# A fused two-layer graph network: tiles that went ahead copied graph by graph, and adj's transposes moved in front of conv1

## The chip, the cores and the metric

The kernel runs on one core of a Trainium2 chip. The metric is the device time of one execution, from the first to the last instruction with what the launch adds around it, in microseconds (us). The core has five engines that work side by side, each on its own list of instructions in order: PE (matrix products and transposes; its weight loads are listed apart as PEld), DVE (vector work), ACT (activations and copies), POOL (vector work and some DMAs) and SP (which issues most DMAs). They meet only through semaphores.

## What is computed

There are 64 graphs of 256 nodes with 256 features each, all in fp32. Layer 0 normalises the adjacency and applies one linear map; layer 1 has a convolution branch over the nodes, a message branch over a distance kernel, and a GRU cell that joins them. Both end in a residual and a layernorm.

```python
# layer 0
deg = adj.sum(-1);  d = where(deg != 0, deg, 1) ** -0.5
a_plus = d[:, :, None] * adj * d[:, None, :] + max(alpha, 1e-10) * eye(N)
x = layernorm(x + (a_plus @ x) @ W.T + b)
# layer 1
h = relu(bn1(conv1(x)))                      # 1 tap: a 256x256 product
h = bn2(conv2(h))                            # 17 taps along the nodes
x_conv = relu(h + x)
s = x @ w_se.T + b_se                        # 3 columns
A = exp(-(|s_n|^2 + |s_m|^2 - 2 s_n.s_m))
msg = relu(x @ w_msg.T + b_msg)
x_nmp = (A * adj) @ msg                      # adj is the mask of layer 1
x = layernorm(x + GRU(cat(x_conv, x_nmp), x))
```

## The kernel before

**Stages.** The 64 graphs are taken in four quarters of 16. Per graph, `layer0` (L335 to 409) makes adj's row sums (ACT), its transposes (`p_adjT`, PE, L367; copied by ACT L368), puts alpha times the degree on the diagonal (DVE L370), scales x by the inverse root of the degree (ACT L380), then makes `hT` (L388) and `p_out` (L398), adds the residual (DVE L403) and takes the layernorm. `layer1` (L411 to 500) transposes the result (`p_x1T`, L419, copied by ACT L420 into `xn`), makes `conv1` together with the three distance columns (`p_conv`, L428), the message product (`p_msg`, L449), the forward transform of the convolution branch (`p_dft`, L463), the distance kernel (`p_rows`, `dist_l`, `dist_r`, `p_dist`, `aT`, L476 to 489) and the aggregation (`p_nmp`, L494). Layer 0 of graph g+2 is woven into layer 1 of graph g.

**The 17-tap convolution** is done through a transform with 48 real coefficients per tile of 32 nodes. The forward transform of all 16 graphs of a quarter lies in one large SBUF tile, `VM` (128 x 48 x 256; `V` is its view by frequency, feature half and tile). `products` then multiplies each frequency by its weights on PE and writes the results back in place, and the transform back also runs in place, on DVE, as a list of small steps: `real_transform`, `complex_begin` and at last `complex_end`, whose steps are called the end steps below. Each of its sixteen `output` pieces ends with a store of 256 KB, `xc_d`, that SP issues (L705). The gates of the quarter read these stores later (`xc_g`, L742).

**Going ahead.** While a quarter's products and its transform back are under way, `VM` is taken. So that PE has something to do, the first graphs of the next quarter go ahead: twelve of them during quarter 0, six during quarters 1 and 2. Their forward transforms go to a second tile, `V2`. When the transform back is done, ACT copies `V2` into `V` in four copies of 12 frequencies each (L1031), and the rest of the graphs, here graphs 28 to 31 for quarter 0, write `V` at once. During quarters 1 to 3 PE also has the gates of the quarter before that were left over (`late`).

**Order.** A scheduler keeps each engine's instructions as the Python program issues them, except for pieces that `issue_after` ties to an instruction. `paced(main, other, rate)` does that for the end steps: after each instruction that called `mark`, it adds `rate` and issues a whole number of steps of `other` behind that instruction. There are six marks per graph: two residual steps L403, two bias steps L431, the message bias L452 and the `aT` product L489. `graphs` walks through the seven pieces of `layer1`, and after each it gives the stages named in `PLACES` one step: piece 0 (after `p_x1T`'s copy) gives to `other`, pieces 1, 4 and 5 to layer 0 of a later graph. In the stages where twelve graphs go ahead `other` is empty.

PSUM has four buffers for these products, used in turn. `V2` lives in a pool of its own that is closed after quarter 0's copies; the gates' tiles take its memory, so the gates' first loads cannot start before the copies have ended.

Of the kernel before, what the change touches and what calls it, by code (L numbers as in the profile page):

```python
# [26 lines left out]
def kernel(  # L27
# [380 lines left out]
        nc.scalar.dma_start(x1_d[g // Q][g % Q].rearrange("(c p) d -> p c d", p=P), x1)  # L408
        yield

    def layer1(g, V, place):  # L411

        x1, adjT = X1.pop(g), ADJT.pop(g)
        xn = work.tile([P, 2 * DCH, N], F32, name="xn")
        x1T = xn[:, :DCH]
        p = bank("p_x1T").rearrange("p (k n) -> p k n", k=DCH)
        for k in range(DCH):
            for c in range(NCH):
                nc.tensor.transpose(p[:, k, c * P : (c + 1) * P], x1[:, c, k * P : (k + 1) * P], ident)  # L419
        nc.scalar.copy(x1T, p)  # L420

        yield

        h = work.tile([P, NCH, D + NSE], F32, name="h", bufs=1)
        for c in range(NCH):
            p = bank("p_conv1")[:, : D + NSE]
            for k in range(DCH):
                nc.tensor.matmul(  # L428
                    p, x1T[:, k, c * P : (c + 1) * P], wc1[:, k, :], start=k == 0, stop=k == DCH - 1
                )  # L430
            mark(nc.vector.tensor_tensor(h[:, c, :], p, bc1, op=ALU.add))  # L431
        nc.scalar.activation(h[:, :, :D], h[:, :, :D], AF.Relu)  # L432

        s3 = h[:, :, D:]
        cols = scols.rearrange("p c (q r) -> p c q r", r=32)
        nc.vector.tensor_copy(cols[:, :, :, :NSE], s3.unsqueeze(2).to_broadcast([P, NCH, 4, NSE]))
        sq3 = small.tile([P, NCH, NSE], F32, name="sq3")
        nc.vector.scalar_tensor_tensor(sq3, s3, -1.0, s3, op0=ALU.mult, op1=ALU.mult)
        nsq = small.tile([P, NCH], F32, name="nsq")
        nc.vector.tensor_reduce(nsq, sq3, AX.X, ALU.add)  # L440
        nc.vector.tensor_scalar(
            cols[:, :, 2:4, NSE], nsq.unsqueeze(2).to_broadcast([P, NCH, 2]), 0.5, None, op0=ALU.mult
        )
        yield
        msg = work.tile([P, NCH, D], F32, name="msg", bufs=1)
        p = bank("p_msg").rearrange("p (c d) -> p c d", c=NCH)
        for c in range(NCH):
            for k in range(DCH):
                nc.tensor.matmul(  # L449
                    p[:, c, :], x1T[:, k, c * P : (c + 1) * P], wmsg[:, k, :], start=k == 0, stop=k == DCH - 1  # L450
                )
        mark(nc.vector.tensor_tensor(msg, p, bmsg_t.unsqueeze(1).to_broadcast([P, NCH, D]), op=ALU.add))  # L452
        nc.scalar.activation(msg, msg, AF.Relu)
        yield


        mid = GT // 2
        for k in range(DCH):
            p = bank("p_dft")

            for c, t0, t1 in ((0, 0, mid + 1), (1, mid - 1, GT)):
                first = t0 + 1 - c * mid
                nc.tensor.matmul(  # L463
                    p[:, t0 * FL : t1 * FL], h[:, c, k * P : (k + 1) * P],
                    fwd[:, first : first + t1 - t0, :].rearrange("p t f -> p (t f)"),
                    start=c == 0, stop=True, skip_group_check=c == 1,
                )
            nc.scalar.copy(
                V[:, :, k, place * GT : (place + 1) * GT],
                p[:, : GT * FL].rearrange("p (t f) -> p f t", f=FL),  # L470
            )

        yield
        p = bank("p_rows")
        for c in range(NCH):
            nc.tensor.transpose(p[:, c * P : (c + 1) * P], scols[:, c, :], ident)  # L476
        dl = work.tile([64, N], F32, name="dist_l", bufs=1)
        nc.scalar.copy(dl, p[0:64, :N])
        dr = work.tile([64, N], F32, name="dist_r", bufs=1)
        nc.vector.tensor_copy(dr, p[64:P, :N])  # L480
        yield

        aT = work.tile([P, NCH, 2, P], F32, name="aT", bufs=1)
        for c in range(NCH):
            rows = slice(32 * c, 32 * c + 32)
            p = bank("p_dist")[:, :N]
            nc.tensor.matmul(p, dl[rows, c * P : (c + 1) * P], dr[rows, :], start=True, stop=True)
            nc.scalar.activation(aT[:, c].rearrange("p n q -> p (n q)"), p, AF.Exp, bias=nsq[:, c : c + 1], scale=2.0)  # L488
        mark(nc.vector.tensor_mul(aT, aT, adjT[:, :, 0:3:2, :]))  # L489
        yield  # L490
        p = bank("p_nmp").rearrange("p (k n) -> p k n", k=DCH)
        for k in range(DCH):
            for mc in range(NCH):
                nc.tensor.matmul(  # L494
                    p[:, k, :], msg[:, mc, k * P : (k + 1) * P], aT[:, mc].rearrange("p n q -> p (n q)"),
                    start=mc == 0, stop=mc == NCH - 1,
                )
        nc.scalar.copy(xn[:, DCH:], p)
        nc.scalar.dma_start(xn_d[g], xn)
        yield  # L500
# [3 lines left out]

    VM = freq.tile([P, FL, D], F32, name="VM")
    V, M = VM.rearrange("p f (k q) -> p f k q", k=DCH), VM

    def load_u(n, i):
        u = ustream.tile([P, DCH, D], F32, name="u")
# [362 lines left out]
    def chain(*stages):  # L872
        for stage in stages:
            yield from stage
# [13 lines left out]
    def run(stage):  # L888
        for _ in stage:
            pass  # L890
# [15 lines left out]

    PLACES = (("other",), ("layer0",), (), (), ("layer0",), ("other", "layer0"), ())

    def graphs(first, part, V, others):


        for i in part:
            load(first + i + 3)
            given = {"layer0": layer0(first + i + 2) if first + i + 2 < B else iter(()), "other": others[i]}
            for piece, _ in enumerate(layer1(first + i, V, i)):
                yield
                for name in PLACES[piece]:
                    if next(given[name], "end") != "end":
                        yield
            yield from given["other"]  # L920

    with tc.tile_pool(name="setup", bufs=1) as setup:
        load_taps(setup, 0)
# [27 lines left out]
        more_weights = gate_weights()  # L951
        others = [weights(setup, i, scale2) for i in range(NPARTS)]
        others += [take(more_weights, 1) for i in range(NPARTS, Q)]
        run(graphs(0, range(Q), V, others))
        bih_t = setup.tile([P, 3 * D], F32, name="bih", tag="taps", bufs=2)
        nc.sync.dma_start(bih_t, bcast_rows(b_ih, 3 * D))
        bhh_t = setup.tile([P, 3 * D], F32, name="bhh", tag="taps", bufs=2)
# [9 lines left out]
    def open_ahead(graphs):  # L967

        scope = ExitStack()
        pool = scope.enter_context(tc.tile_pool(name="ahead", bufs=1))  # L970
        return scope, graphs, pool.tile([P, FL, DCH, graphs * GT], F32, name="V2")
# [17 lines left out]
    def nothing():  # L989
        return iter(())  # L990

    RATES = (1.2, 0.85, 0.85, 1.35)


    scope, AHEAD, V2 = open_ahead(12)
    late = nothing()
    for q in range(NQ):
        first = (q + 1) * Q
        more = q + 1 < NQ
        end = complex_end(q)  # L1000
        if more:
            if q:
                others = [take(late, 3 if i % 3 == 0 else 2) for i in range(AHEAD)]
            else:
                others = [nothing() for _ in range(AHEAD)]
            begin = graphs(first, range(AHEAD), V2, others)
        sums(0)
        real = real_transform()
        for step in range(STEPS):
            if step < 4:  # L1010
                run(products(step))
            else:
                run(merge(products(step), take(real, 1)))
                run(complex_begin(step))
            if q:
                run(take(late, (0, 1, 1, 1, 1, 1, 2, 1, 2, 1, 2, 1)[step] if more else step % 2))
            else:
                run(take(begin, 3))
        run(real)
        if not q:  # L1020
            run(paced(begin, end, RATES[q]))
        elif more:
            run(paced(chain(merge(take(late, 20), take(begin, 6), 3), begin), end, RATES[q]))
        else:
            run(paced(late, end, RATES[q]))
            run(end)
        if more:
            run(late)
            run(end)
            for f in range(0, FL, 12):  # L1030
                nc.scalar.copy(V[:, f : f + 12, :, : AHEAD * GT], V2[:, f : f + 12])  # L1031
            if q == 0:
                scope.close()
                gate = ctx.enter_context(tc.tile_pool(name="gate", bufs=2))
            early = gates(q, range(EARLY))
            others = [take(early, 5 if q == 0 else 2) for _ in range(Q)]
            run(graphs(first, range(AHEAD, Q), V, others))
            run(early)
            if q == 0:
                scope, AHEAD, V2 = open_ahead(6)  # L1040
                ctx.enter_context(scope)
            late = gates(q, range(EARLY, Q))
        else:
            run(gates(q, range(Q)))
# [53 lines left out]
```

## Time and profile before

| | us |
|---|---|
| median of three runs | 2169.46 (2168.36 to 2170.78) |
| the profiled execution | 2174.33 |
| its span, first to last instruction | 2172.5 |
| mean granted TensorE clock | 0.989 of full speed |

The stages of the span, with the time in which PE was busy:

| stretch, us | what runs | PE busy |
|---|---|---|
| 0 to 540 | setup, the first quarter's graphs, its products and transform back | 489.74 of 540 |
| 540 to 700 | first gates, graphs 29 to 31, on to the second quarter's products | 153.44 of 160 |
| 700 to 1000 | second quarter, its transform back and copies (968 to 974) at the end | 289.02 of 300 |
| 1000 to 1300 | the same on to the third quarter | 296.14 of 300 |
| 1300 to 1700 | its transform back, on to the fourth | 386.44 of 400 |
| 1700 to 1940 | the fourth quarter's transform back beside gates | 226.12 of 240 |
| 1940 to 2172 | the last gates | 223.11 of 232 |

Graph 28, the first after those that went ahead in quarter 0, has its `p_conv` at 529.61 us; the last store of quarter 0's transform is issued at 519.92, and the first gate load at 529.10. The twelve graphs that go ahead are 16 to 27.

In a timeline a line has the start, the duration, the engine, the line of the kernel, the operation, what it writes and reads with its shape, the number of instructions in the group, and in brackets the idle time just before it with the engine and line that ended it. In a table of windows the columns are the busy time and instruction count of each engine in the stretch, then the granted clock of PE, the share of DMA time and the rate in GB/s. Releasers are worked out from semaphores: where several were waited for, the last is named.

### The profile page before, as it was taken

Reading aid. Unit: us, or ns where it says so; the run is one execution under the profiler, and the core shown is the slowest. Engines: PE = TensorE matmul, PEld = TensorE weight load, DVE = VectorE, ACT = ScalarE, POOL = GpSimd, SP = SyncE. Lnnn points to the kernel's source line nnn. Section 1 sums busy time; section 2 is a strip of 40 time slices with the busy share of each in tenths; the row PEclk is TensorE's granted clock in tenths of the full one; section 3 lists DMA queues with packets and bytes.
Section 4 is the critical chain, followed back from the end, with each engine's and each line's share of the span. In section 5 each row is a group of like instructions: output and inputs, shape, how many; then the busy total and the mean of one; then the engine's idle time right before and its main releaser. Section 6 shows DMA issues by size and latency. Waiting matters only on the chain. (4 is left out here: it accounts for less than half of the span.)

```text
span 2172.5 us, 29034 instructions
## 1 busy us (share of the span) xinstructions
PE 2064.0 (95%) x9805; PEld 1748.4 (80%) x9805; DVE 1550.7 (71%) x3691; ACT 834.3 (38%) x1847; POOL 664.2 (31%) x640
## 2 busy tenths in 40 slices
PE   7999999887999999999999999899999998999998
PEld 5788788776788887788888888778888887788887
DVE  5555568785568798775556989775555889977776
ACT  4566643455331122455453122346543112222222
POOL 2444310211431233313222133323231123444442
PEclk9999999999999999999999999999999999999999
DMA  4765656434337644344335754334334844444442
GB/s 129 223 194 178 216 185 207 154 125 141 97 112 226 194 123 122 107 119 121 104 99 175 208 163 116 110 117 132 101 97 124 250 117 122 120 123 107 112 101 60
DMA packets 251182, 305.65 MB, mean 141 GB/s; under 512 B 18174, under 2 KB 229714, under 8 KB 251034
## 3 DMA queue, kind: packets, MB, share of 16 engines
q1 hardware_dynamic: 183530, 200.46, 30.4%
q10 hardware_dynamic: 44480, 67.39, 8.7%
q0 software_dynamic: 23024, 35.95, 8.6%
q8 instruction: 78, 1.28, 0.2%
q14 instruction: 70, 0.57, 0.1%
HBM read 200.62 MB, written 103.06 MB: 140 GB/s over the span
## 5 line engine op out<-in xcount | busy, mean ns | idle before, releaser
L833 PE MATMUL p_n<-wn,inputs 128*128 128x256 f32 x1536 | 355.9, 385 | 11.0 <-DVE first L809 10.6
L796 PE MATMUL p_rz<-wrz,sums 128*128 128x256 f32 x1536 | 350.9, 382 | 3.2 <-POOL sums L775 2.3
L833 PEld LDWEIGHTS p_n<-wn,inputs 128*128 128x128 f32 x1536 | 289.1, 192 | 58.1 <-DVE first L809 14.5
L796 PEld LDWEIGHTS p_rz<-wrz,sums 128*128 128x128 f32 x1536 | 290.7, 191 | 48.2 <-issue 5.9
L796 PE MATMUL p_rz<-wrz,inputs 128*128 128x256 f32 x1152 | 271.7, 379 | 0.4 <-ACT inputs L766 0.4
L314 POOL TENSOR_TENSOR ln_rs<-ln_rs,neg_half 128x2 f32<-128x2 f32 x129 | 101.2, 784 | 527.9 <-DVE ln_rs L313 417.4
L796 PEld LDWEIGHTS p_rz<-wrz,inputs 128*128 128x128 f32 x1152 | 217.5, 190 | 30.3 <-ACT inputs L766 1.0
L845 ACT ACTIVATE nn<-gn 128x256 f32<-128x256 f32 x128 | 53.2, 416 | 333.2 <-DVE gn L842 333.0
L518 PE MATMUL p_k<-u,VM 128*128 128x256 f32 x736 | 175.3, 380 | 4.1 <-DMA u<-ud 3.3
L775 POOL TENSOR_TENSOR sums<-inputs 128x384 f32<-128x384 f32 x64 | 67.8, 1059 | 335.1 <-ACT inputs L766 327.0
L358 POOL TENSOR_TENSOR dis<-deg,neg_half 128x2 f32<-128x2 f32 x64 | 46.5, 726 | 402.6 <-DVE deg L356 395.6
L324 ACT ACTIVATE x_g<-x_g,ln_mr,ln_rs 128x256 f32<-128x256 f32 x128 | 70.0, 593 | 245.6 <-DVE ln_mr L322 242.0
L518 PEld LDWEIGHTS p_k<-u,VM 128*128 128x128 f32 x736 | 138.1, 190 | 25.7 <-DMA u<-ud 3.4
L428 PE MATMUL p_conv<-wc,xn 128*128 128x259 f32 x512 | 128.8, 394 | 19.6 <-ACT xn L420 18.5
L388 PE MATMUL p_hT<-adjT,x 128*128 128x256 f32 x512 | 126.6, 390 | 9.5 <-DVE msg L452 4.9
L381 POOL TENSOR_TENSOR x_t<-x_t,b_t 128x512 f32<-128x512 f32 x64 | 86.4, 1350 | 146.7 <-ACT x L380 89.3
L463 PE MATMUL p_dft<-fwd,h 128*128 128x240 f32 x512 | 117.8, 373 | 13.9 <-ACT h L432 13.0
L428 PEld LDWEIGHTS p_conv<-wc,xn 128*128 128x128 f32 x512 | 97.1, 194 | 39.8 <-ACT xn L420 24.1
L489 DVE TENSOR_TENSOR aT<-aT,adjT 128x512 f32<-128x512 f32 x64 | 44.3, 692 | 115.3 <-ACT aT L488 115.3
L398 PE MATMUL p_out<-w,hT 128*128 128x256 f32 x512 | 123.9, 385 | 2.5 <-ACT hT L393 2.1
L449 PE MATMUL p_msg<-wmsg,xn 128*128 128x256 f32 x512 | 121.3, 379 | 0.0
L494 PE MATMUL p_nmp<-aT,msg 128*128 128x256 f32 x512 | 121.1, 379 | 0.2 <-DVE aT L489 0.2
(154 smaller groups left out, 3894.9 us busy)
## 6 DMA issues: line engine op xcount, KB each, us to landing
u<-ud SPq DMA_DIRECT2D x284, 256.0 KB
xn_d<-xn ACTq DMA_DIRECT2D x64, 512.0 KB
inputs<-xn_d SPq DMA_DIRECT2D x64, 512.0 KB
ud<-u_set POOLq DMA_DIRECT2D x39, 480.0 KB, 6.2
adj_t<-in_adj_dram SPq DMA_DIRECT2D x64, 256.0 KB
x_t<-in_x_dram SPq DMA_DIRECT2D x64, 256.0 KB
x_d<-x ACTq DMA_DIRECT2D x64, 256.0 KB
xc_d<-VM SPq DMA_DIRECT2D x64, 256.0 KB
```

Source lines behind the costliest of these rows:

```text
L314: nc.gpsimd.tensor_tensor(rs[:, : len(chunks)], rs[:, : len(chunks)], neg_half[:, : len(chunks)], op=ALU.pow)
L324: nc.scalar.activation(y[:, c, :], y[:, c, :], AF.Identity, bias=mr[:, c : c + 1], scale=rs[:, c : c + 1])
L381: nc.gpsimd.tensor_tensor(x_t, x_t, b0_t.unsqueeze(1).to_broadcast([P, NCH, D]), op=ALU.add)
L388: nc.tensor.matmul(p[:, k, :], x1[:, mc, k * P : (k + 1) * P], adjT[:, mc, 1 - mc : 3 - mc, :].rearrange("p n q -> p (n q)"), start=mc == ...
L398: nc.tensor.matmul(p[:, c, :], hT[:, k, c * P : (c + 1) * P], w0[:, k, :], start=k == 0, stop=k == DCH - 1)
L428: nc.tensor.matmul(p, x1T[:, k, c * P : (c + 1) * P], wc1[:, k, :], start=k == 0, stop=k == DCH - 1)
L449: nc.tensor.matmul(p[:, c, :], x1T[:, k, c * P : (c + 1) * P], wmsg[:, k, :], start=k == 0, stop=k == DCH - 1)
L463: nc.tensor.matmul(p[:, t0 * FL : t1 * FL], h[:, c, k * P : (k + 1) * P], fwd[:, first : first + t1 - t0, :].rearrange("p t f -> p (t f)") ...
L494: nc.tensor.matmul(p[:, k, :], msg[:, mc, k * P : (k + 1) * P], aT[:, mc].rearrange("p n q -> p (n q)"), start=mc == 0, stop=mc == NCH - 1,)
L518: nc.tensor.matmul(p[:, j * D : (j + 1) * D], v[:, k, :], u[:, k, :], start=k == 0, stop=k == DCH - 1)
L796: nc.tensor.matmul(p[:, j * D : (j + 1) * D], a[:, k], wrz[:, b, k], start=k == 0, stop=k == HALF - 1)
L833: nc.tensor.matmul(p[:, o * D : (o + 1) * D], lhsT, w, start=j == 0, stop=j == len(part) - 1)
```

## The change

Three things change. First, `V2` is copied graph by graph: a new generator, `copies`, has one ACT copy per graph that wrote to `V2`, and it is chained to the end steps, so that `paced` places its copies as it places those. `TILES[0]` says which tile `layer1` writes its forward transform to; `copies` sets it to `V` when it starts, so a graph that comes to its transform afterwards writes `V` directly, and `AWAY` lists the graphs that did not. In the order that results, quarter 0 has eleven copies (graph 27 writes `V`), and quarters 1 and 2 five each. Second, the rates of the end steps in quarters 0, 1 and 2 rise, from 1.2, .85, .85 to 1.4, .9, .9. Third, `graphs` takes layer 0's first piece (row sums, transposes, diagonal, scale) after piece 0 where `other` has nothing there, instead of after piece 1. That moves it in front of `conv1` for the twelve graphs during quarter 0 and for no others. The number of instructions changes on ACT alone, by nine more.

```diff
-    def layer1(g, V, place):
+    def layer1(g, place):
...
         mid = GT // 2
+        if TILES[0] is not V:
+            AWAY.append(place)
         for k in range(DCH):
...
             nc.scalar.copy(
-                V[:, :, k, place * GT : (place + 1) * GT],
+                TILES[0][:, :, k, place * GT : (place + 1) * GT],
...
     V, M = VM.rearrange("p f (k q) -> p f k q", k=DCH), VM
+    TILES, AWAY = [V], []
...
-    def graphs(first, part, V, others):
+    def graphs(first, part, others):
         for i in part:
             load(first + i + 3)
-            given = {"layer0": layer0(first + i + 2) if first + i + 2 < B else iter(()), "other": others[i]}
-            for piece, _ in enumerate(layer1(first + i, V, i)):
+            zero = layer0(first + i + 2) if first + i + 2 < B else iter(())
+            begun = False
+            for piece, _ in enumerate(layer1(first + i, i)):
                 yield
                 for name in PLACES[piece]:
-                    if next(given[name], "end") != "end":
+                    if name == "other" and next(others[i], "end") != "end":
                         yield
-            yield from given["other"]
+                    elif piece == 0:
+                        begun = next(zero, "end") != "end"
+                        yield
+                    elif name == "layer0" and not (piece == 1 and begun) and next(zero, "end") != "end":
+                        yield
+            yield from others[i]
...
-    RATES = (1.2, 0.85, 0.85, 1.35)
+    RATES = (1.4, 0.9, 0.9, 1.35)
...
+    def copies(V2):
+        waiting = list(AWAY)
+        AWAY.clear()
+        TILES[0] = V
+        for i in waiting:
+            nc.scalar.copy(V[:, :, :, i * GT : (i + 1) * GT], V2[:, :, :, i * GT : (i + 1) * GT])
+            yield
...
-        end = complex_end(q)
+        end = chain(complex_end(q), copies(V2) if more else iter(()))
...
-            begin = graphs(first, range(AHEAD), V2, others)
+            TILES[0] = V2
+            begin = graphs(first, range(AHEAD), others)
...
             run(late)
             run(end)
-            for f in range(0, FL, 12):
-                nc.scalar.copy(V[:, f : f + 12, :, : AHEAD * GT], V2[:, f : f + 12])
```

## The prediction

> **What bounds the kernel now.** I read the page's busy shares first, then busy time by stage, then the waits of PE and of DVE in the stage that changes, then the timelines at its end.
>
> ```profile
> span 2172.5 us, 29034 instructions
> ## 1 busy us (share of the span) xinstructions
> PE 2064.0 (95%) x9805; PEld 1748.4 (80%) x9805; DVE 1550.7 (71%) x3691; ACT 834.3 (38%) x1847; POOL 664.2 (31%) x640
> ```
>
> PE sets the time: 108.5 us of 2172.5 are left to gain, and an edit to ACT's copies or to DVE's order counts only where PE stands still. Windows by stage, 402 to 521.4 us being the main loop of quarter 0 and 521.4 to 543 the seam behind it:
>
> ```profile
> core 0: us, PE busy (x) PEld busy (x) DVE busy (x) ACT busy (x) POOL busy (x), PEclk, DMA share, GB/s
> 288.00:402.00 114.00, 111.34 (x535) 94.96 (x534) 86.37 (x195) 40.53 (x89) 11.00 (x12) 1.00 0.66 210
> 402.00:521.40 119.40, 103.12 (x498) 81.58 (x497) 95.65 (x287) 67.79 (x154) 24.84 (x24) 1.00 0.38 122
> 521.40:543.00 21.60, 13.93 (x63) 11.32 (x62) 5.83 (x22) 12.84 (x22) 5.12 (x5) 0.84 0.67 192
> ```
>
> PE lacks 16.3 us in the stage and 7.7 in the seam, and the seam's clock is 0.84. The waits between 400 and 522 us (engine line waited for: total, times, longest), of PE and of DVE:
>
> ```profile
> PE p_conv L428 <- ACT xn L420: 5.8, 8, 0.7
> PE p_dist L487 <- DVE dist_r L480: 2.5, 4, 0.8
> PE p_hT L388 <- DVE adjT L370: 2.3, 2, 1.5
> PE p_hT L388 <- DVE msg L452: 1.9, 2, 1.1
> ...
> DVE aT L489 <- ACT aT L488: 16.4, 9, 2.8
> DVE ln_mr L322 <- POOL ln_rs L314: 4.9, 8, 0.7
> DVE dist_r L480 <- ACT dist_l L478: 3.0, 4, 1.0
> ```
>
> PE waits for DVE in three places; DVE never waits for PE directly, only for short round trips. So DVE, 95.65 of 119.4 us busy and idle only in such trips (24.3 in all), carries this stage, and PE's 5.8 us before p_conv are mostly slack that it would spend a little later. The seam, on PE and then ACT (start, duration, group, idle before and its releaser):
>
> ```profile
> 517.82 1.99 PE L398 MATMUL p_out<-w,hT 128*128 128x256 f32 x8 [1.33 <-ACT hT L393]
> ...
> 521.38 0.60 PE L419 MATMUL p_x1T<-ident,x 128*128 128x128 f32 x4
> 529.61 3.59 PE L428 MATMUL p_conv<-wc,xn 128*128 128x259 f32 x8 [7.63 <-ACT xn L420]
> 533.03 0.60 PE L367 MATMUL p_adjT<-ident,adj_t 128*128 128x128 f32 x4
> ```
>
> ```profile
> 515.17 2.12 ACT L1031 COPY VM<-V 128x2304 f32<-128x2304 f32 x1
> ...
> 520.07 2.10 ACT L1031 COPY VM<-V 128x2304 f32<-128x2304 f32 x1
> ...
> 524.95 4.12 ACT L1031 COPY VM<-V 128x2304 f32<-128x2304 f32 x2 [0.58 <-ACT x L324]
> 528.98 0.58 ACT L420 COPY xn<-p_x1T 128x512 f32<-128x512 f32 x1
> ```
>
> PE stands 7.63 us because xn of graph 28 is queued behind the last two block copies. The conv then starts its successor 3.42 us later instead of 1.86 (403.36 to 405.22, 418.44 to 420.30): 1.56 us lost to the lower clock.
>
> **What the Trainium skill says.** "TensorE: Matmul & The Clock Gate", Part 1, *What's actually happening*: PE falls to half clock after an idle window of about 3.4 us and needs about that much busy time to return; the window runs free. The trace agrees (granted clock .50 just after the 7.63), and shows .54 after a wait of only 1.90 at 549.76 us, while waits of 1.5 and 1.62 left it whole. The specification table of that page gives ScalarE a strict in-order queue: a copy that waits holds everything behind it, as in the seam. "ScalarE: Activation LUTs", *What ACT_TABLE_LOAD costs*: 186 ns + 0.833 ns per element for an ACTIVATE without pointers. The trace's copies agree: 512 elements 0.58, 2304 elements 2.12. "DMA: Bandwidth & Descriptors", *Anatomy of one DMA*, puts most of a transfer's fixed cost into the wait for the write's receipt (written of POOL's DMAs); here a 256 KB load that SP issued at 529.10 let POOL go at 532.12, so I take 3.0 us from issue to landing for the output stores too.
>
> **The change part by part.**
>
> *Copies by graph and faster end steps, quarter 0.* Before, 4 copies of 12 frequencies follow the transform back. After, 11 copies of one graph do (128x768, estimate 186 + 640 = 0.83 us each); graph 27, the twelfth, writes V at once. ACT's sum is 9.1 us against 8.3, so the point is place, not work. The end steps on DVE finish one graph earlier: 16 of them, 0.35 us apart in the timeline, 5.6 us, move ahead of dist_r of graph 26. That stood at 500.35; some 1.6 us of the 5.6 fall into waits for POOL ln_rs (0.6 each), so it comes at 504.35, just behind the last end step. Then:
> - Each copy covers all frequencies, so the first waits for all of DVE's last steps and for the last stores, to about 504.4 + 3.0 = 507.4; before, only the third copy did. Behind it on ACT stand hT, the two aT, layer 0's scales and xn. It ends at 508.2, hT at 508.75, and p_out, which stood at 502.05, starts there: PE, +4.0 late from dist_r, waits some 2.5 us more.
> - conv of graph 27 comes at 514.05 instead of 506.93, 7.1 late. Graph 27 now has no end steps, so PE sets it: 12.9 us. Further copies stand ahead of its msg and DFT copies (3 and 2, each 0.83, partly in ACT's idle time): p_dist waits an estimated 2.35, p_nmp 0.4.
> - conv of graph 28: 514.05 + 12.9 + 2.75 = 529.7, against 529.61. The stall is cut into pieces rather than removed, since DVE had to do its 5.6 us of end steps in any case and PE has nothing else to fill with.
> - What goes for certain is the half clock after 7.63 us: −1.56. Two waits of 2.3 to 2.5 us may bring it back, between 0 and +3.4; I take +0.6.
> - Gate loads start 3.5 us earlier (copies end at 525.6, not 529.07). p_xcT waited for nothing at 543.16, so 0. Its successor's 1.90 us wait for POOL's sums at 549.76 stays.
>
> Sum: +0.1 − 1.56 + 0.6 = −0.9.
>
> *adj's transposes between x1T and conv1.* This happens for 12 graphs, those that go ahead in quarter 0. In the 8 with a 0.73 us gap before p_conv, transposes of 0.44 fill it: −3.5 at most, nothing where DVE is late anyway. ACT now takes adjT's copy and the two L380 scales ahead of relu h, and DVE its two L370 ahead of scols: h by 0.25 to 0.75 later, for a p_dft that waited 1.19 once in this stage. Bounds −3.5 and +1.5; I take −0.3, for the first graphs only, where DVE has no end steps queued. No PE instruction is added.
>
> *Quarters 1 and 2.* Each has 5 copies (4.2 us) instead of 4 of 1152 (4.4). Before, they cost PE nothing (968.12 and 971.43 us), as late gate matmuls fill PE; so 0, with +1.5 each if that fill is gone. The rate of .9 for .85 puts 4 more end steps, 1.4 us, ahead of the dist_r that PE already waits 4.87 us for at 854.99; .7 to 1.3 of it falls into ln_rs waits, so +0.4. In return end steps finish earlier, and waits of .31 (945.9) and .45 (982.3) go: −0.76. Net −0.4 each, −1.5 to +2.0. Quarter 3 is untouched.
>
> *Total.* −0.9 − 0.3 − 0.8 = −2.0. The profiled run took 2174.33 us: its span of 2172.5 and 1.8 around it. It becomes 2172.3. The three timed runs have the median 2169.46, 4.9 lower; the difference carries over: **2167.5**, written as 2167.
>
> **Rivals.**
> 1. *PE is the bound after all, and the stall goes.* For it: 7.63 + 1.33 of idle time and 1.56 of clock hang on ACT's order alone, and 5.8 us of PE waits stand exactly where transposes come in. Against: DVE's waits show no PE. If ACT is never late again the seam gives 10.5 less the usual 0.73 before a conv, −9.8, and half the adjT bound would add −1.7; against that stands one copy's 0.83 in front of hT, twice: −9.8 → 2159.7.
> 2. *The first graph's copy blocks ACT: slower.* Place: ACT's queue in graph 26 and 27, where hT and aT stand behind a copy that waits for the last store. Price: each us of landing beyond 3.0 is a us of PE, and the stalls, beyond 3 us each, halve the clock twice. For it: DMA share is .42 in 505 to 521 us and .67 in the seam, and a 1.90 wait already cost clock. Against: the stores are spread over the last steps. With landing at 5.0: −0.9 + 2.0 + 2.8 of clock, −0.3 for adjT, and the same copy holds ACT in quarters 1 and 2 by 1.0 each, without their gain: +5.6 → 2175. It decides from a landing of about 4.5 us on.
> 3. *Nothing arrives.* The order puts the copies where the old ones ended and the clock drops as before: 2169.5. The instruction order speaks against it: the copies do stand in graph 27.
>
> **How the numbers follow.** Forecast .50, rival 1 .24, rival 2 .20, rival 3 .06. About 0.2%, 4.3 us, is what a measurement of this kernel can tell from no change. The forecast's own range from the bounds above (−1.56 or +1.9 in the seam, −3.5 to +1.5, −3 to +4) is 2162 to 2172. Under 2165.1 lie rival 1 and a third of the forecast: .40. Over 2173.8 lie rival 2 and a little of the forecast: .22. The rest, .38, is the same. The range 2159 to 2174.5 takes in most of rival 1 and half of rival 2.
>
> **What would show it.** Right: PE's waits from 500 to 530 us still sum to about 5 to 8 us, but as two or three of 2 to 3 us, with p_out late behind a 768-element copy; conv1 of graph 28 within a us of 529.6, and its successor 1.86 us later; dist_r's wait near 855 us at 4.9 to 5.5. Wrong, to the good: graph 28's conv at 522 us, or the gaps before conv1 shrinking and the graphs' period with them (15.1 and 14.5 us from 403.36 on). Wrong, to the bad: a wait over 4 us in front of p_out with a clock of .5 behind it, or new PE waits near 968 us.

## The result, and the profile after

The changed kernel is slower. Seven timed runs have the median 2177.73 us (2174.54 to 2179.87), those of the kernel before 2170.11 (2168.36 to 2172.79). The ratio is 1.0032, with a 95% interval of 1.0020 to 1.0043: about 7 us more, where 2 us less was forecast and 2174.5 was the upper end of the range.

The two profiled executions don't show this at first sight: their spans are 2172.8 and 2172.5 us. The profiled execution before was above all seven timed runs of its kernel (2174.33), and the one after is of the fastest run of its own (2174.54). Besides, they differ by 2.9 us already at graph 4, where both kernels issue the same instructions. So the spans are no comparison; stretches are a better one, if one looks at the clock in them too (last section). The table takes the start of the first p_nmp matmul of a graph in each trace, less that in the trace of before, and less the same at graph 15, the last before the first change. A plus is lateness, in us. Graphs 16 to 27 go ahead in quarter 0, 28 to 31 follow the seam, 32 to 37 go ahead in quarter 1, 48 to 53 in quarter 2.

```
graph                    15    19    23    27    31    32    36    47    48    52    63
after                   0.0   0.1   4.9   7.4  -1.7   0.1   2.5   1.4   2.7   5.2   4.2
```

The seam wins back what the twelve graphs lost and 1.7 more, as the prediction had it within 0.5, but not for its reasons (see below). Then quarter 1 loses 4.2 us from graph 31 to 36 and quarter 2 3.8 from 47 to 52, and each gives back about 1.

Windows of after, for the stretches shown of before (columns as there):

```profile
402.00:521.40 119.40, 99.42 (x467) 77.44 (x465) 91.24 (x274) 68.16 (x153) 23.73 (x24) 0.99 0.37 120
521.40:543.00 21.60, 20.71 (x94) 16.72 (x93) 9.63 (x32) 12.34 (x31) 6.56 (x7) 0.92 0.70 203
```

PE now has 20.71 us of work in the second window instead of 13.93, and 99.42 instead of 103.12 in the first: idle time has moved forward. Two of its waits from 400 to 545 us before, and those after:

```profile
PE p_conv L428 <- ACT xn L420: 13.4, 9, 7.6
...
PE p_dft L463 <- ACT h L432: 1.2, 1, 1.2
```

```profile
PE p_dft L465 <- ACT h L432: 7.9, 7, 2.5
PE p_dist L489 <- DVE dist_r L482: 4.5, 5, 1.8
PE p_conv L428 <- ACT xn L420: 3.0, 9, 0.7
PE p_out L398 <- ACT hT L393: 2.3, 1, 2.3
```

The 13.4 us in front of p_conv, 7.63 of them at the seam, have become 3.0. In their place p_dft waits 7.9 us for relu h; before, it was 1.2. The seam on PE:

```profile
506.66 1.99 PE L398 MATMUL p_out<-w,hT 128*128 128x256 f32 x8 [2.26 <-ACT hT L393]
...
520.87 0.70 PE L489 MATMUL p_dist<-dist_r,dist_l 32*128 32x256 f32 x4 [1.81 <-DVE dist_r L482]
...
528.09 2.02 PE L428 MATMUL p_conv<-wc,xn 128*128 128x259 f32 x8 [0.73 <-ACT xn L420]
```

The large stall is cut into waits of 2.26 and 1.81, the first behind a copy of 768 elements in ACT's queue, and graph 28's conv is at full clock again. Last, PE's waits from 780 to 990 us, in quarter 1, before and then after:

```profile
PE p_dist L487 <- DVE dist_r L480: 5.8, 2, 4.9
```

```profile
PE p_dist L489 <- DVE dist_r L482: 5.8, 3, 4.7
PE p_n L836 <- DVE first L812: 2.6, 2, 1.5
PE p_dft L465 <- ACT h L432: 2.4, 4, 0.8
```

The wait for dist_r that the prediction watched is as long as it was. A new one stands in front of it: p_n, the gates' product, waits 2.6 us for DVE's `first`, which before was never late here.

### The profile page after: what moved, and what is told of

Read it like the earlier page. It is cut to its first block, busy times and chain, and to the rows that moved or that the text cites. A ratio compares the mean times of both kernels' runs of the same rounds, so it can differ in the third digit from the quotient of the medians.

```text
span 2172.8 us, 29029 instructions
## 1 busy us (share of the span) xinstructions
PE 2063.7 (95%) x9805; PEld 1746.5 (80%) x9805; DVE 1556.5 (72%) x3691; ACT 832.4 (38%) x1856; POOL 663.0 (31%) x640
## 4 chain that ended last, share of the span: by engine, by line
PE 49%; DVE 14%; issue 7%; POOL 6%; ACT 4%; DMA 1%; ACTq 0%; POOLq 0%; DVEq 0%
PE p_rz L799 19%; PE p_n L836 9%; PE p_k L521 7%; PE p_out L398 3%; PE p_nmp L496 2%; PE p_dft L465 2%; PE p_hT L388 2%; PE p_msg L449 2%; PE p_conv L428 1%; POOL ln_rs L314 1%; PE p_dist L489 1%; POOL xc_g L756 1%; POOL sums L778 1%; POOL sums L779 1%; ACT inputs L769 1%
## 5 line engine op out<-in xcount | busy, mean ns | idle before, releaser
L465 PEld LDWEIGHTS p_dft<-fwd,h 128*128 128x128 f32 x512 | 95.3, 192 | 44.8 <-ACT h L432 38.3
```

The lines of the kernel that those rows point to most:

```text
L465: nc.tensor.matmul(p[:, t0 * FL : t1 * FL], h[:, c, k * P : (k + 1) * P], fwd[:, first : first + t1 - t0, :].rearrange("p t f -> p (t f)") ...
```

## The experiments

Eighteen kernels were run, in five groups, each group with its own executions of the kernel before. So kernels are compared by their ratio, and medians only within a group. The rates stand for quarters 0, 1 and 2; "a/b" means rate a in the first part of quarters 1 and 2, where late gates are merged with graph 32's (48's) first pieces, and b behind it. "Move" is adj's first piece in front of conv1.

| run | copies | move | rates | us, median | ratio to before, 95% |
|---|---|---|---|---|---|
| the change | by graph | yes | 1.4, .9 | 2177.73 | 1.0032 (1.0020 to 1.0043) |
| noT | by graph | no | 1.4, .9 | 2174.01 | 1.0016 (1.0007 to 1.0025) |
| r12old | by graph | yes | 1.4, .85 | 2168.26 | 0.9986 (0.9978 to 0.9994) |
| noT_r12old | by graph | no | 1.4, .85 | 2165.23 | 0.9972 (0.9961 to 0.9982) |
| T_only | old | yes | 1.2, .85 | 2174.42 | 1.0012 (1.0004 to 1.0021) |
| copies_only | by graph | no | 1.2, .85 | 2168.63 | 0.9983 (0.9977 to 0.9990) |
| r12_only | old | no | 1.2, .9 | 2181.17 | 1.0041 (1.0029 to 1.0053) |
| q12_80 | by graph | no | 1.4, .8 | 2166.41 | 0.9983 (0.9976 to 0.9990) |
| q0_16 | by graph | no | 1.6, .85 | 2169.26 | 0.9992 (0.9985 to 0.9998) |
| r_first | by graph | no | 1.4, .9/.85 | 2175.18 | 1.0020 (1.0012 to 1.0027) |
| r_second | by graph | no | 1.4, .85/.9 | 2165.53 | 0.9977 (0.9967 to 0.9986) |
| r_70_100 | by graph | no | 1.4, .7/1.0 | 2174.20 | 1.0012 (1.0003 to 1.0021) |
| r_80_90 | by graph | no | 1.4, .8/.9 | 2162.25 | 0.9953 (0.9940 to 0.9966) |
| phase | by graph | no | 1.4, .85, count from ½ | 2175.01 | 1.0017 (1.0010 to 1.0023) |
| T_PE | by graph | PE's part | 1.4, .85 | 2166.33 | 0.9975 (0.9966 to 0.9985) |
| T_copy | by graph | PE and adjT's copy | 1.4, .85 | 2166.00 | 0.9974 (0.9965 to 0.9984) |
| T_split | by graph | all but the scales | 1.4, .85 | 2168.91 | 0.9989 (0.9983 to 0.9996) |
| T_scales_back | by graph | all but the scales | 1.4, .85 | 2167.22 | 0.9986 (0.9980 to 0.9993) |
| T_diagonal_back | by graph | all but the diagonal | 1.4, .85 | 2172.44 | 1.0010 (1.0003 to 1.0017) |

### Which of the three parts makes the loss

```diff
@@ noT: the change, its piece 0 taken out
-                    elif piece == 0:
-                        begun = next(zero, "end") != "end"
-                        yield
@@ r12old: the change; noT_r12old has both
-    RATES = (1.4, 0.9, 0.9, 1.35)
+    RATES = (1.4, 0.85, 0.85, 1.35)
```

T_only is the kernel before with the change's `graphs`.

> The changed kernel, with adj's transposes back behind conv1. Theory R (the rates .9 in quarters 1 and 2 cost some 3 us each, because end steps now stand on DVE in front of work that PE waits for): the time stays near the changed kernel's, 2177 us, +6 to +7.5 against the kernel before; in the trace the steps of +3 us per quarter remain. Theory T (the transposes' move puts relu h behind two scales on ACT, and p_dft's wait for h rises from 1.2 to 7.9 us between 400 and 545 us): 4 us faster than the changed kernel, about +3.5 against before; p_dft's waits fall back to 1 to 2 us and p_conv's for xn rise to about 6. Theory C (the copies by graph cost it): as R.

> The changed kernel with rates .85 in quarters 1 and 2 as before, 1.4 in quarter 0. Theory R: 6 us faster than the changed kernel, about +1 against the kernel before; from graph 31 to graph 47 the aggregation p_nmp keeps its distance to the kernel before within 0.5 us, where the changed kernel lost 3.2. Theory T: no change, +7. Theory C: at most 1 us gained, the distance still grows by 2 to 3 us per quarter, after the copies.

> The changed kernel with both undone: transposes behind conv1 and .85 in quarters 1 and 2; what stays are the copies by graph and 1.4 in quarter 0. Theories R and T together: -3 against the kernel before (2167). R alone: +1. T alone: +3. Theory C: +5 or more.

> The kernel before with adj's transposes in front of conv1, nothing else. Theory T: +4 against the kernel before, with p_dft's waits for relu h at 6 to 8 us between 400 and 545 us. Theories R and C: within 1 us of the kernel before. If PE rather than DVE sets those graphs: -3.5.

Then two parts alone: copies_only is noT with `RATES = (1.2, 0.85, 0.85, 1.35)`, r12_only is the kernel before with `RATES = (1.2, 0.9, 0.9, 1.35)`.

> The kernel before with the copies by graph alone: transposes behind conv1, rates 1.2, .85, .85, 1.35 as before. If the copies themselves bring the gain of 5.5 us that copies and rate 1.4 showed together: -4 to -5.5 against the kernel before (2165 to 2167). If the rate of 1.4 in quarter 0 is what brings it, since at 1.2 the twelve copies end as late as the old ones: within 1.5 us of the kernel before (2169 to 2172), with a PE wait over 6 us in front of p_conv of graph 28.

> The kernel before with .9 instead of .85 in quarters 1 and 2, nothing else. Theory R: +9 against the kernel before (2179 to 2180), as between the two runs that differ in this alone, with new p_n waits for DVE first of 1 us or more in both quarters. If the rate hurts only together with the copies by graph: within 2 us of the kernel before.

The parts add up. Of .9 instead of .85 there are three pairs: the ratios 1.0032 over 0.9986, 1.0016 over 0.9972, and 1.0041 alone are 1.0046, 1.0044 and 1.0041, some 9.5 us. The move costs 1.0016, 1.0014 and 1.0012 in its three pairs, some 3 us. Copies by graph with 1.4 in quarter 0 gain 6 (0.9972). Together 9.5 + 3 − 6 = 6.5, against 7 measured. Of the gain, the copies alone make 0.9983; the rest, about 2.4 us, is the rate of 1.4, though the two intervals just overlap. Theory C falls: the copies are what helps. The granted clock is no rival for the rate's loss: its mean over the timed runs is 0.0002 to 0.0004 lower with .9 in the three pairs (0.9912 against 0.9916 in noT and noT_r12old), at most 0.9 us of the 9.5 (an estimate: the difference times the span of 2172 us). The traces show the same in place (as in the table above):

```
graph                    15    19    23    27    31    32    36    47    48    52    63
noT                     0.0   0.0   2.1   5.3  -1.5   0.0   2.3   2.6   3.6   6.0   5.0
r12old                  0.0   0.1   5.0   7.8  -1.4  -2.9  -2.8  -3.6  -3.9  -4.0  -4.8
noT_r12old              0.0   0.8   2.8   6.2  -3.3  -3.9  -3.9  -4.9  -4.6  -4.7  -5.5
T_only                  0.0   0.6   2.8   5.0   4.2   4.1   4.1   4.0   3.6   3.6   3.6
copies_only             0.0   0.0   0.0  -1.3  -1.2  -1.0  -0.7  -1.4  -1.4  -1.4  -2.1
r12_only                0.0   0.0   0.1   0.9   0.2   2.6   5.0   4.8   6.3   8.7   8.8
```

r12_only is the kernel before up to graph 31 and stands 0.2 us from it there; at graph 36 it is 5.0 late, at 52 8.7. Nothing but end steps that DVE takes sooner is different.

### How a rate of .9 can cost 9 us

```diff
@@ r_first (.9, .85), r_second (.85, .9), r_70_100 (.7, 1.0), r_80_90 (.8, .9): noT, with
+    def then(rate, by):
+        rate[0] = by
+        return
+        yield
...
-            run(paced(chain(merge(take(late, 20), take(begin, 6), 3), begin), end, RATES[q]))
+            rate = [RATES[q]]
+            run(paced(chain(merge(take(late, 20), take(begin, 6), 3), then(rate, 0.85), begin), end, rate))
@@ phase: noT_r12old, shortened, with
-        due = 0
+        due = 0.5        # in quarters 1 and 2
```

q12_80 and q0_16 are noT with other numbers in `RATES`.

> Copies by graph, transposes behind conv1, rates 1.4, .8, .8, 1.35: the steps of quarters 1 and 2 stretched further than before. If the loss at .9 is a slope (end steps in front of DVE work that PE waits for), another .05 less gives 2 to 4 us more: 2161 to 2163, with the p_dist wait of 4.78 us near 849 us smaller. If .85 was already past the point where DVE holds PE up, the steps left over pile up behind the last graphs and the time is 2165 to 2170, with new PE waits from 960 us on.

> Copies by graph, transposes behind conv1, rates 1.6, .85, .85: quarter 0's end steps end one graph earlier still. If the seam's remaining waits come from the first copy's wait for the last store, they move to a graph whose work hides them no better: 2164 to 2167, no change. If a further graph without end steps gives PE time back: 2162 to 2164.

> As the run without the move and with .85 in quarters 1 and 2 (2165.2), but the rate is .9 in the first part of those quarters, where twenty pieces of late gates are merged with graph 32's first six pieces, and .85 behind it. 4 more end steps stand in front of dist_r of graph 32, as at .9 throughout. Theory that the first part makes the loss (p_n waits for DVE first): +6 to +8, 2171 to 2173, with p_nmp of graph 32 later by 3 us or more. Rival, that graphs 33 to 36 make it: within 2 us, 2165 to 2167.

> The same with .7 in the first part of quarters 1 and 2 and 1.0 behind it: 8 end steps fewer in front of dist_r of graph 32, the same number done (212 instead of 210) at graph 36. Theory that the place of the steps counts: p_dist's 4.8 us wait near 849 us falls by about 2.8, graphs 33 to 36 give a part of it back: 2160 to 2164. Rival, that the sum over both parts is fixed since DVE is the bound in both: 2165 within 1.5.

> Copies by graph, no move, rates 1.4, .85, .85, with the count of due steps starting at one half instead of zero in quarters 1 and 2: 2 end steps more in front of dist_r of graph 32 (150 instead of 148), and every later step behind another of the marked instructions. If the number of steps in front decides: 2 x 2 steps of 0.35 us, +1 to +2, 2166 to 2167. If the place behind one mark or another decides as much as the number, the time moves by more than that, +4 or more, with waits of DVE for ACT trz of 3 us instead of 2.4 in front of dist_r.

> Rates .8 in the first part of quarters 1 and 2 and .9 behind it: 146 end steps in front of dist_r of graph 32 (148 at .85), and 164, 180, 194, 212 at graphs 33 to 36 (166, 180, 194, 210 at .85). If dist_r of graphs 32 and 48 comes 2.3 and 2.9 us earlier, as at .8 throughout, and graphs 33 to 36 lose nothing, since as many steps are done by then: 2160 to 2162. If the place of the steps in graphs 33 to 36 costs as in the other runs that left .85: 2164 to 2167.

> Rates .85 in the first part of quarters 1 and 2 and .9 behind it. If the rate's loss of 9 us is made in the first part alone: 2165 to 2166.5. If half of it is made in graphs 33 to 36, as the traces at .9 look: 2168 to 2171.

q12_80 missed in total: no gain over .85. Its trace says why: dist_r of graph 32 comes 2.3 us earlier and that of 48 2.9, but from graph 34 to 37 5.4 us are lost, where the steps left over pile up (206 of 216 done at graph 36, against 210). Of these, 1.7 us are clock: PE's granted clock falls to half (0.50) for 3.41 us at graph 35, and again at graph 51. q0_16 is 4 us slower than 1.4, so a further graph without end steps gives nothing and there is an optimum there as well.

The split rates tell where the loss begins: r_first is as slow as .9 throughout (1.0020 and 1.0016), r_second as fast as .85 (0.9977 and 0.9972). It is all set off in the first part. But it isn't all spent there. r_first's dist_r of graph 32 is 1.6 us later than noT_r12old's, measured from graph 31 (p_nmp only 0.7, since noT_r12old had half clock for 6.8 us behind that wait and r_first for 3.4), and by graph 36 another 1.8 is gone, at the same rate as noT_r12old has behind graph 32. What it carries along is where the steps fall.

One thing that this place decides is which of DVE's instructions run beside POOL's. Over graphs 33 to 36 noT loses 2.4 us on noT_r12old, with the clock at 1.00 in both. DVE's long instructions there (over 0.15 us above the median of the same instruction in noT_r12old) exceed that median by 8.2 us in noT and by 5.8 in noT_r12old, and all of them, 10 and 8, ran beside a POOL instruction. The difference is as large as the loss; but no run moves POOL's work, so that it makes the loss isn't shown.

The run phase shows the weight of the place by itself. Its rate is .85, and it has two end steps more in front of dist_r of graph 32, 0.7 us of work. It loses 10 us (1.0017 against 0.9972), as much as .9, though a part of that is clock: its mean over the timed runs is 0.0012 lower, by the same estimate 2.6 us. In the trace it falls to half for 3.41 us at graph 34 and at graph 50, where noT_r12old's does not, 1.7 us each.

```
graph                    15    19    23    27    31    32    36    47    48    52    63
phase                   0.0   0.9   3.0   6.4  -3.2  -1.1   1.8   1.1   2.9   5.7   5.0
r_80_90                 0.0   0.0   2.0   5.8  -3.9  -7.8  -6.5  -7.3 -11.3 -10.1 -10.7
```

Here are DVE's instructions around one `first`, that of the same graph, in the trace of noT_r12old and then of phase (turn and VM are end steps; the gates' L812, L819, L841 and L859 call `mark` too, besides the six marks that each graph has, so steps are also placed behind these):

```profile
786.62 0.69 DVE L861 TENSOR_TENSOR x_g<-x_g,nn 128x512 f32<-128x512 f32 x1
...
788.10 0.66 DVE L812 TENSOR_TENSOR first<-p_rz,brz_t 128x512 f32<-128x512 f32 x1
...
789.14 0.42 DVE L602 SCALAR_TENSOR_TENSOR turn<-VM 128x256 f32<-128x256 f32 x1
790.17 0.16 DVE L322 SCALAR_TENSOR_TENSOR ln_mr<-ln_mv,ln_rs 128x2 f32<-128x2 f32 x1 [0.61 <-POOL ln_rs L314]
```

```profile
779.46 4.17 DVE L842 SCALAR_TENSOR_TENSOR gn<-trz,gn 128x256 f32<-128x256 f32 x1
...
785.49 0.41 DVE L707 SCALAR_TENSOR_TENSOR VM<-turn,VM 128x256 f32<-128x256 f32 x1
785.82 0.41 DVE L842 SCALAR_TENSOR_TENSOR gn<-trz,gn 128x256 f32<-128x256 f32 x1
786.16 0.41 DVE L707 SCALAR_TENSOR_TENSOR VM<-turn,VM 128x256 f32<-128x256 f32 x1
786.49 0.41 DVE L845 SCALAR_TENSOR_TENSOR gn<-gn 128x256 f32<-128x256 f32 x1
787.39 0.69 DVE L860 SCALAR_TENSOR_TENSOR nn<-trz,nn 128x512 f32<-128x512 f32 x1 [0.48 <-ACT nn L848]
...
789.59 0.66 DVE L812 TENSOR_TENSOR first<-p_rz,brz_t 128x512 f32<-128x512 f32 x1
```

A step between gn and nn makes everything up to `first` later, and DVE still stops for ACT's nn behind it. A step behind `first` overlaps the round trip to POOL. In this one gate the same steps cost their whole length in one place and part of it in the other. The first line of phase is an instruction of 0.41 us that took 4.17 beside POOL's sums (L779 to L783); in noT_r12old three instructions took 1.2 us each there. On PE, in phase:

```profile
790.30 5.45 PE L836 MATMUL p_n<-wn,inputs 128*128 128x256 f32 x24 [1.32 <-DVE first L812]
```

In noT_r12old no p_n wait is listed in this stretch. Over 751 to 849 us DVE's idle time for ACT trz is 2.4 us in noT_r12old and 4.1 in phase:

```profile
DVE x_g L859 <- ACT trz L823: 2.4, 4, 1.1
```

```profile
DVE x_g L859 <- ACT trz L823: 4.1, 4, 1.2
```

r_70_100 fell short of its expectation. It has 12 steps fewer than .9 in front of dist_r of graph 32, but the waits for trz are 4.6 us there, and dist_r comes no earlier than in noT_r12old (0.2 us later, from graph 31 on). Its p_nmp of graph 32 is 2.3 us earlier all the same, and that is clock: behind the wait it fell to half in noT_r12old and stayed whole in r_70_100 (p_dist, four matmuls, 1.22 against 0.70 us).

```profile
849.26 1.22 PE L489 MATMUL p_dist<-dist_r,dist_l 32*128 32x256 f32 x4 [4.78 <-DVE dist_r L482]
```

```profile
848.00 0.70 PE L489 MATMUL p_dist<-dist_r,dist_l 32*128 32x256 f32 x4 [3.38 <-DVE dist_r L482]
```

Graphs 33 to 36 lose 3.0 us again; in quarter 2, where r_70_100's clock fell too, there is no gain at all. In r_80_90 the steps are fewer and dist_r does come earlier, by 2.5 and 2.7 us: its wait is 2.9 us instead of 4.8 (PE, graph 32), and as many steps as at .85 are done by graph 36 (212 against 210). Of the 3.3 and 4.2 us that it gains on noT_r12old up to p_nmp of graph 32 and of 48, 0.9 and 1.6 are clock again, half for 3.4 us behind the shorter wait instead of 6.8.

```profile
846.33 0.70 PE L489 MATMUL p_dist<-dist_r,dist_l 32*128 32x256 f32 x4 [2.93 <-DVE dist_r L482]
```

It beats both kernels: 2162.25 us in five timed runs, 0.9953 of the kernel before (0.9940 to 0.9966), some 10 us less.

### What the move of adj's first piece costs

```diff
@@ layer0, in r12old: T_PE yields here, between the transposes and their copy
         for mc in range(NCH):
             for c in range(NCH):
                 nc.tensor.transpose(...)
+        if split:
+            yield
         copied = nc.scalar.copy(adjT[:, :, 0:3:2, :], ...)
```

T_copy yields behind `copied`, T_split behind the diagonal, in front of the scales. Their second half is issued after relu h. T_scales_back is T_split without the extra yield to the products' loop; T_diagonal_back issues the scales in front of relu h and the diagonal behind it.

> As the run with rates 1.4, .85, .85 and the transposes moved, but only row sums, transposes, their copy and the diagonal stand in front of conv1; the two scales of x come behind relu h, as before the change. Theory that h behind the two scales makes the move's loss: the 3 us come back, 2165 or a little less, p_dft's waits for h at 2 to 4 us instead of 8. Rival, that the diagonal on DVE ahead of the columns and the message makes it: no gain, 2168.

> Copies by graph and rates 1.4, .85, .85, as the run without the transposes' move that took 2165.2, but with the four transposes of adj on PE in front of conv1; their copy on ACT, the diagonal on DVE, the scales and POOL's part stay behind conv1 and relu h. If DVE sets those graphs, filling PE's gap brings nothing: 2164.5 to 2166. If what ACT and DVE do earlier made the 3 us loss and the gap on PE is worth something: 2162 to 2164. If the loss comes from the transposes themselves (a PSUM buffer taken earlier): 2168.

> As the run in which PE's transposes alone were moved (2166.3), with their copy on ACT moved too; the diagonal on DVE (two instructions of 0.3 us, in front of the columns and the message) and the scales stay behind relu h. If the diagonal on DVE makes the move's loss of 3 us: 2165 to 2166.5. If the copy on ACT makes it: 2168 to 2169.

> Rates 1.4, .85, .85 and the transposes' move, with the two scales behind relu h, and without the side effect of the first such run, which also moved graphs 17 to 19 against the products of quarter 0. Diagonal in front of the columns on DVE, scales on ACT behind relu h. If the diagonal makes the move's loss: 2168 to 2169 as with the whole move. If the scales in front of relu h make it: 2165 to 2166, and p_dft's waits for h fall to half of 8 us.

> The same with the diagonal behind relu h and the scales left in front of it. If the diagonal makes the loss: 2165 to 2166. If the scales make it: 2168 to 2169. If neither alone does, both runs lie between, near 2167.

With PE's transposes alone, or with their copy as well, the ratio is that of the kernel without the move (0.9975 and 0.9974 against 0.9972): filling PE's 0.44 us in front of each conv shows no cost and no gain. But T_PE and T_copy, like T_split, have one more yield per graph, which changes when graphs 17 to 19 run beside the products, and that may have helped them. T_split differs from T_copy by the diagonal alone and is some 3 us slower (0.9989, the intervals just overlapping). Its trace is 4.7 us late by graph 19, by one wait of 3.46 us and the half clock behind it (2.9 of the 4.7), in which p_dft takes 3.57 us instead of 1.89.

```profile
395.30 3.57 PE L467 MATMUL p_dft<-fwd,h 128*128 128x240 f32 x8 [3.46 <-ACT h L434]
```

With the scales put back and no further yield, p_dft's waits for h fall as the theory of the scales says, from 8.0 us to 4.8 between 395 and 545 us:

```profile
PE p_dft L467 <- ACT h L434: 4.8, 7, 2.1
```

But the ratio, 0.9986 (0.9980 to 0.9993), is that of the whole move, 0.9986, so nothing is clearly won. With the diagonal put back and the scales in front it is 1.0010, 5 us worse than with the whole move. T_split and T_scales_back speak for the diagonal, T_diagonal_back against it; but that run is no clean test either, since of the 7.3 us that its trace is behind r12old's at graph 31, 5.0 are half clock. Which of the two makes the loss isn't settled.

The traces show what the sums of p_dft's waits hide. PE's whole idle time from graph 15 to 31 is no longer with the move (29.0 and 29.1 us in after and r12old, 27.6 to 30.8 in the eight traces with the same copies and no move): p_dft waits where p_conv waited before. What is added is half clock. In all four traces with the scales in front of relu h, graph 20's p_dft waits 2.15 to 2.48 us and then runs at half clock, 3.27 to 3.52 us long; in the sixteen others it takes 1.89. r12old and then T_scales_back:

```profile
405.40 3.52 PE L465 MATMUL p_dft<-fwd,h 128*128 128x240 f32 x8 [2.47 <-ACT h L432]
```

```profile
409.06 1.89 PE L467 MATMUL p_dft<-fwd,h 128*128 128x240 f32 x8 [2.08 <-ACT h L434]
```

Over the timed runs the mean clock is 0.0005 to 0.0007 lower with the move in its three pairs, by the same estimate 1.1 to 1.5 us of the 3; the rest stays open.

## Why the prediction was wrong

**The rate in quarters 1 and 2 is where it failed.** The step read: 4 more end steps, 1.4 us, in front of dist_r, ".7 to 1.3 of it falls into ln_rs waits, so +0.4", and nothing else. The three pairs give about 4.7 us in each quarter, outside the stated bound of +2.0. Two things were wrong. The count of steps was priced against one wait, dist_r's; but DVE is behind in the whole stretch, and what is issued in front of `first`, relu h and the columns makes PE late at each of them. From noT_r12old to noT dist_r's wait at graph 32 stays at 4.7 to 4.8 us; p_n's waits for `first` grow from 0 to 2.1 us in front of it, and p_dft's for h from 1.1 to 2.5 in graphs 33 to 36. And the credit for idle time was assumed: the steps don't go where the idle time is, they go behind marks. From noT_r12old to the changed kernel's rate (noT), dist_r of graph 32 comes 2.2 us later from graph 31 on, not 0.1 to 0.7, and graphs 33 to 36, which the prediction put at nothing, add 2.4.

**The copies' tail in those quarters was right in size, by luck.** −0.76 was forecast because end steps would finish earlier at .9 and the waits of .31 and .45 go. r12old and noT_r12old drop by 0.75 to 0.89 between graphs 36 and 38 and again from 52 to 54, but at .85, and copies_only drops too, while r12_only, with .9 and the old copies, gains 0.2 at most and keeps the wait of .45. So it is the copies by graph that win it. The wait of .31 is still there in noT_r12old and is .56 in noT.

**The seam had the right mechanism and too small a gain.** The first copy did stand behind the last steps (it starts at 505.29, 3.1 us after DVE's last end step ended and the last store was issued, both at 502.2; 3.0 was taken; that it waits for the store is inferred, as the profile does not name what released it), p_out's wait was 2.26 (2.5 forecast), p_dist's 1.81 (2.35), and the stall came apart rather than away. But the sum of copies and rate 1.4 in quarter 0 is −3.3 us in noT_r12old's trace at graph 31, not −0.9. The term mis-sized is the clock. Before, PE had half clock for 10.2 us at the seam (from 526.00, 6.83, and from 549.89, 3.41), and its work took 3.3 us longer for it. The prediction took back 1.56 of this, put in +0.6 for the pieces, and left the second stretch in place; it had copied the order around it and not asked whether that drop would come again. In noT_r12old's trace the waits of 1.61, 2.69 and 1.98 leave the clock whole, and the second stretch is gone too. That is in part luck: eight of the traces have the same instructions up to graph 31. Five of them have no half clock there and stand at −3.2 to −4.5; three have 10.2 us of it, as before, and stand at −2.0 to +0.7, about the −0.9 of the forecast on average. Over the timed runs the mean clock rises from 0.9889 to 0.9916 with the copies and 1.4, by the same estimate up to 5.9 us, so most of what the two gain may be clock. In the changed kernel itself it fell to half for 3.41 us from 522.55, behind the wait of 1.81.

**The move was priced at −0.3, and costs 3.** Its upper bound of +1.5 was taken from h being late by 0.25 to 0.75 behind the scales, "for a p_dft that waited 1.19 once". It waits in seven graphs now, and behind the longest of these waits comes a stretch of half clock, which had no term in the sum. The reading that PE's gap before conv is no gain since DVE sets those graphs fits T_PE; the same reading should have warned that an instruction put in front of others on DVE or ACT there can make PE late.

In quarter 0 the two errors nearly cancel, by luck: −1.2 forecast, −1.7 in the trace. The stated range was also too narrow for its own bounds: they add up to 2176.9 at the top, not 2172, which is still below the 2177.73 measured. And one step of the seam's working doesn't follow: p_out at 508.75 instead of 502.05 is 6.7 us late, yet graph 27's conv behind it was put 7.1 late. Rival 2 had the right sign for another cause: the first copy's wait isn't what costs. Rival 1's seam came out in part.

## What to carry to other kernels

Where a second engine is behind the first in a whole stretch, count its instructions in front of every one that the first engine waits for, not of the one that waits longest. Work that is threaded in at a rate has two numbers, how much and behind which instruction; moving the start of the count by one half cost as much here as the rate itself, so a rate has to be tried, together with its phase and by stage, and a good value isn't a slope to follow. Ask too what the moved work will run beside, and put a term for the clock behind every wait of PE of about 2 us and more. When an engine has slack in front of an instruction, look at what shares the other engines' order with the filler before filling it.

## What the runs showed of the hardware

**The clock.** The traces record two values of the granted clock here, whole and half. Half clock comes in stretches of 3.41 us or two or three times that (the last one is cut off by the end of the trace), and within a trace all edges lie on one grid of 3.41 us. A mean such as the .54 of the prediction mixes the two. The clock doesn't follow the length of one wait, but how much of a grid window PE is busy. Here is one p_conv, in noT and then in noT_r12old, after the same wait:

```profile
507.87 3.58 PE L428 MATMUL p_conv<-wc,xn 128*128 128x259 f32 x8 [2.69 <-ACT xn L420]
```

```profile
511.31 2.02 PE L428 MATMUL p_conv<-wc,xn 128*128 128x259 f32 x8 [2.69 <-ACT xn L420]
```

In noT the wait lies in one window (504.24 to 507.65, PE busy 0.93 us of 3.41), and the next is at half clock. In noT_r12old it is split between two (busy 2.34 and 1.79 us), and the clock stays whole. Over all twenty traces, from 61 us on, 12117 windows of the grid had whole clock. All 83 in which PE was busy for less than 0.4 of the time were followed by half clock, none of the 11840 over 0.6, and 32 of the 194 between. The Trainium skill's free-running window of about 3.4 us ("TensorE: Matmul & The Clock Gate", Part 1, *What's actually happening*) agrees with the grid. The window that it calls idle need not be idle, though: PE was busy for 1.14 us of the one in front of 549.89 in the kernel before, and for 1.68 us of the one in front of 522.55 in the changed kernel. Where the grid falls differs between executions of the same instructions, and their times with it, by more than the effects sought. So only medians, or stretches with the clock beside them, can be compared.

**DVE beside POOL.** In the twenty traces 2674 DVE instructions took over 0.3 us more than the median of the same instruction in their trace, and every one of them overlapped a POOL instruction. A `gn` of 0.41 us took 1.2, once 4.17; an L370 of 0.35 took 1.35.
